# Expert results gathered row by row for each token, and one group's routing held behind two quads of expert tiles

## The chip, the cores and the metric

The kernel runs on one core of a Trainium2 chip (trn2). The metric is device time in microseconds (us) of one launch, as the median of several runs. TensorE (PE) multiplies matrices, VectorE (DVE) and ScalarE (ACT) work on elements, GpSimd (POOL) copies weights and issues indirect DMAs, SyncE (SP) issues the plain ones.

## The reference

Sixteen sequences of 256 tokens with 128 features pass through half a mixture-of-experts layer, an attention layer, and half an expert layer again with the same weights.

```python
x = x + 0.5 * _L0_ffn_ref(_layernorm(x, axis=-1), norm_scale, gate_w, gate_b, w1, b1, w2, b2)
x = x + _L0_attn_ref(_layernorm(x, axis=-1), Wq, bq, Wk, bk, Wv, bv, Wfq, bfq, Wfk, bfk)
x = x + 0.5 * _L0_ffn_ref(_layernorm(x, axis=-1), norm_scale, gate_w, gate_b, w1, b1, w2, b2)

# _L0_ffn_ref, 32 experts, 4 for each token, t the normalized rows
g = t @ gate_w.T + gate_b
vals, idx = jax.lax.top_k(gf, K)
w = jax.nn.softmax(vals, axis=-1)
combine = jnp.zeros((T, E)).at[jnp.arange(T)[:, None], idx].add(w)
h1 = jnp.einsum('th,efh->tef', tf, w1) + b1
h = _swiglu(h1)
out = jnp.einsum('tef,ehf->th', h * combine[:, :, None], w2) + combine @ b2
return x + out
```

## The kernel before

The 4096 tokens form two groups of four blocks; a block (`TB`) is four token tiles of 128 tokens. Each group goes through the layer twice with experts: `first[g]` and `last[g]` hold the state of the first and the second pass (tile names end in `_f` and `_l`).

**Routing.** `route` normalizes a block, computes the gates, finds the best four experts, and keeps the mask `m`, the rank of each token among those of its tile that chose the same expert (`rank`), and the weights (`combT`). `dispatch` turns the counts into places: each expert's tokens of one tile are put into rows of five (`RB = 5`), a row of 640 floats being one unit of the scratch memory `xs` (sorted inputs) and `ys` (expert outputs). One-hot matmuls (line 677) build the rows and one indirect DMA a token tile (line 596, on POOL) scatters 128 rows of 2560 bytes.

**Experts.** `experts` walks over 23 quads (`NQS`) of four expert tiles of 25 rows each. For a quad it loads `xq` (line 710, SP), copies the four tiles' first weights from the resident `w_sb` into the buffers `w1` (line 717, POOL, five buffers, two used by a quad), transposes `xq`, multiplies (`ph`, line 737), applies the gate function on ACT and DVE (lines 741, 742, 747), multiplies again (`po`, line 755), and stores `ys` (line 762, SP). After each quad it calls `beside`, which takes a few steps of another generator.

**Beside.** `groups` runs four expert passes, each next to one chain: `enter(1)` (route and dispatch group 1), `middle(0)` and `middle(1)` (combine the first pass, attention, route and dispatch the second pass), `leave(0)` (combine the second pass and store). `leave(1)` comes last, next to nothing. The number of steps a quad is 3, 3, 3, 2. Inside a chain, `staggered` starts the blocks some steps apart.

```python
beside = [enter(1, clear), middle(0), middle(1), leave(0)]
steps = [3, 3, 3, 2]
for i in range(2 * n_grp):
    waiting.append(beside[i])
    st = first[i] if i < n_grp else last[i - n_grp]
    experts(st, 0, nq, lambda: step(steps[i]))
    finish()
waiting.append(leave(1))
finish()
```

**Combine.** `combined` gathers, for each token tile, the tile's 128 rows of `ys` with one indirect DMA (line 786, POOL, four buffers `gt` of 128 x 640 floats). On PE it forms the places of all pairs in the rows (`pa`, lines 798 and 799) and the weights (`pwb`, line 800), on DVE ten weighted one-hot matrices `u` (line 809), and it multiplies them with the gathered rows: five `pu` matmuls a token tile (line 816) and one for the biases `b2` (line 819). The residual is added at line 822. It is called for every block of both passes.

The order in which the instructions of an engine are issued is fixed when the kernel is built: the framework takes those that are ready by its own estimates, earlier written ones first, and adds the semaphores. The last part of the kernel, under `tc.If`, is a second run for token counts that don't fit into 23 quads; it does not run with these inputs.

Of the kernel before, what the change touches and what calls it, by code (L numbers as in the profile page):

```python
# [13 lines left out]
I32 = mybir.dt.int32  # L14
AF = mybir.ActivationFunctionType
# [7 lines left out]
P = 128  # L23
NJ = 4
# [22 lines left out]
NB = NT * BT  # L47
LIMIT = 7.0
# [3 lines left out]
NONE = -1.0e38  # L52
ROUND = 8388608.0
# [3 lines left out]
def kernel(  # L57
# [144 lines left out]

    ones = const.tile([P, P], BF16, tag="ones", name="ones")
# [197 lines left out]
    class Group:  # L401


        def __init__(self, g, name):
            self.g, self.name = g, name
            self.blocks = []
            self.n = grp.tile([P, GB], BF16, tag="n", name=f"n_{name}", bufs=3)
            self.row = grp.tile([P, 2, GJ], U32, tag="row", name=f"row_{name}", bufs=3)
# [5 lines left out]
        def enter(self, b):  # L414
            self.blocks.append(Block())
            self.held(b, "tn", [P, NJ, P], F32, GB + 1)
            self.blocks[b].xr = dram.tile(
                [P, NJ * P], F32, tag=f"xr_{self.name}{b}", name=f"xr_{self.name}{b}"
            )

            self.held(b, "rank", [P, P], BF16, 2 * GB + 2)
            self.held(b, "combT", [P, P], F32, 2 * GB + 2)
            return self.blocks[b]

        def sort(self, b):
            self.held(b, "seg", [P, P], F32, 2 * GB + 2)
            self.held(b, "seg_b", [P, P], BF16, 2 * GB + 2)
            self.held(b, "off", [P, P], BF16, 2 * GB + 2)
            return self.blocks[b]
# [14 lines left out]
    def route(st, src, b, co):  # L444
# [11 lines left out]
        pt = transposed(tn, f"pt_{name}")  # L456
# [18 lines left out]
        for j in range(NJ):  # L475
# [3 lines left out]
        comb = small.tile([P, NJ, NE], F32, tag="comb", name=f"comb_{name}")  # L479
# [9 lines left out]
            upto_self.rearrange("p c t -> p (c t)"), start=True, stop=True,  # L489
        )  # L490
# [35 lines left out]
    def dispatch(st, clear=False):  # L526
# [45 lines left out]
        )  # L572
        pick = small.tile([P, GB, 2 * NJ], F32, tag="pick", name=f"pick_{name}")
# [116 lines left out]

    def loaded(tab, q, engine, top):
        _, vals = nc.values_load_multi_w_load_instructions(
            tab[0:1, q * NJ : (q + 1) * NJ], engines=[engine],
            min_val=0, max_val=top, skip_runtime_bounds_check_because="made on the chip from at most NE - 1",
        )
        return vals

    def experts(st, lo, hi, beside):
# [28 lines left out]
        def first(q):  # L727
# [4 lines left out]
            for c in range(2):  # L732
                ph = ps_h.tile([P, 2, 2, P], F32, tag="ph", name=f"ph_{name}_{q}_{c}")
                ts = slice(2 * c, 2 * c + 2)
                for s in range(2):
                    for part in range(2):
                        nc.tensor.matmul(  # L737
                            ph[:, part, s, 0:RT], w_q[c][:, s, part * P : (part + 1) * P],
                            x_q[:, 2 * c + s, :], start=True, stop=True,
                        )  # L740
# [33 lines left out]
    def combined(st, b, tag):  # L774
# [47 lines left out]
        nc.vector.tensor_tensor(r, pu, xr, ALU.add)  # L822
        yield r
# [116 lines left out]

    first, last = {}, {}
# [21 lines left out]
    def routes(g, gap, most):  # L963
# [6 lines left out]
        yield  # L970

# [174 lines left out]
```

## Time and profile before

| | |
|---|---|
| median of 3 runs | 738.46 us (733.2 to 739.15) |
| profiled execution | 734.1 us, of which the span of the trace is 732.0 us |
| PE, DVE, ACT, POOL busy | 620.1, 483.1, 379.5, 284.5 us |
| mean granted clock of PE | 0.938 |
| first and last `ph_f` matmul | 99.6 and 378.8 us |
| first and last `ph_l` matmul | 407.2 and 683.1 us |
| gathers (line 786) | 64, 0.94 to 1.44 us each on POOL |
| scatters of rows (line 596) | 64, and 9 that clear rows |
| weight copies (line 717) | 368, 0.416 us in the mean |

An engine's busy time is what its instructions take; waiting at a semaphore is not in it. For an indirect DMA the entry on POOL is the issuing of it, not the transfer. A PE matmul of 32-bit floats shows as two records here (320 records of line 816 for the 160 matmuls of two groups). A row of a timeline gives start, duration, engine, line, operation, what is written and read, and in brackets the idle time ahead of it with what ended it.

### The profile page before, as it was taken

The numbers are of one execution on the slowest core, as the hardware profiler recorded it, in microseconds if no ns is written. First come the engines' busy times: TensorE is split into PE (matmuls) and PEld (weight loads), VectorE is DVE, ScalarE is ACT, GpSimd is POOL, SyncE is SP. The second block draws the span as 40 slices with busy tenths as digits, with TensorE's granted clock in tenths as the row PEclk, the third lists the DMA queues.
The fourth block names the chain that finished last, engine by engine and source line by source line (L and its number), as shares of the span: only waits on it lengthen the run. The fifth ranks groups of instructions, "written<-read, shape, count | busy, mean of one in ns | idle before, by whom it ended". The sixth has DMA issues, their size and how long they took to land.

```text
span 732.0 us, 15990 instructions
## 1 busy us (share of the span) xinstructions
PE 620.1 (85%) x4897; PEld 574.3 (78%) x4897; DVE 483.1 (66%) x1823; ACT 379.5 (52%) x902; POOL 284.5 (39%) x567
## 2 busy tenths in 40 slices
PE   3677489979978988988997998988889789999595
PEld 1466389878978977977896887877789689999585
DVE  6863975855555688887774469888878535554443
ACT  2753376735543766864552455775655335445210
POOL 3023424467645422122365532402227645434242
PEclk9887779999999999998999999999999989999989
DMA  7999346477656435124355644513434667765463
GB/s 229 374 336 328 138 139 172 128 259 227 193 157 198 128 90 140 48 81 128 112 197 194 185 119 124 143 44 85 129 100 174 215 182 213 199 189 160 111 204 118
DMA packets 132695, 122.45 MB, mean 167 GB/s; under 512 B 9626, under 2 KB 118714, under 8 KB 132602
## 3 DMA queue, kind: packets, MB, share of 16 engines
q1 hardware_dynamic: 117658, 71.62, 34.6%
q0 software_dynamic: 10960, 44.90, 18.2%
q10 hardware_dynamic: 3984, 4.82, 1.8%
q8 instruction: 43, 0.70, 0.4%
q14 instruction: 50, 0.41, 0.2%
HBM read 57.78 MB, written 63.52 MB: 166 GB/s over the span
## 4 chain that ended last, share of the span: by engine, by line
PE 53%; DVE 21%; DMA 11%; ACT 7%; issue 6%; POOL 1%; another core or an unknown queue 0%; SPq 0%; POOLq 0%; ACTq 0%; DVEq 0%
PE ph_l L737 8%; PE ph_f L737 7%; PE p_l L677 4%; PE pu_f L816 4%; PE po_l L755 4%; PE po_f L755 4%; PE p_f L677 3%; PE pu_l L816 3%; DMA xs<-s_f,row_f 3%; PE pxT_l L723 2%; DMA gt_l<-ys,row_l 2%; DMA xq_l<-xs 1%; DMA w_sb<-in_w_dram 1%; PE pxT_f L723 1%; DVE lin_f L742 1%
## 5 line engine op out<-in xcount | busy, mean ns | idle before, releaser
L717 POOL COPY w_l<-w_sb 128x256 f32 x184 | 71.3, 416 | 124.4 <-PE ph_l L737 118.6
L717 POOL COPY w_f<-w_sb 128x256 f32 x184 | 70.3, 414 | 117.7 <-PE ph_f L737 116.2
L737 PE MATMUL ph_f<-xT_f,w_f 128*128 128x125 f32 x736 | 97.7, 281 | 1.4 <-DVE lin_f L742 1.1
L737 PE MATMUL ph_l<-xT_l,w_l 128*128 128x125 f32 x736 | 95.5, 279 | 0.1
L737 PEld LDWEIGHTS ph_f<-xT_f,w_f 128*128 128x128 f32 x736 | 90.9, 197 | 2.4 <-POOL w_f L717 1.4
L737 PEld LDWEIGHTS ph_l<-xT_l,w_l 128*128 128x128 f32 x736 | 89.6, 196 | 0.6 <-issue 0.3
L742 DVE TENSOR_SCALAR lin_l<-ph_l 128x250 f32<-128x250 f32 x92 | 37.8, 413 | 53.8 <-ACT a_l L741 53.3
L742 DVE TENSOR_SCALAR lin_f<-ph_f 128x250 f32<-128x250 f32 x92 | 37.5, 412 | 37.3 <-ACT a_f L741 36.2
L816 PE MATMUL pu_l<-gt_l,u_l 128*128 128x128 f32 x320 | 46.2, 290 | 11.5 <-DMA gt_l<-ys,row_l 7.5
L816 PEld LDWEIGHTS pu_l<-gt_l,u_l 128*128 128x128 f32 x320 | 42.7, 203 | 16.8 <-issue 9.8
L677 PE MATMUL p_f<-tn_f,o_f 128*128 128x128 f32 x320 | 46.3, 303 | 10.2 <-DVE rank_f L438 4.1
L677 PEld LDWEIGHTS p_f<-tn_f,o_f 128*128 128x128 f32 x320 | 43.1, 214 | 14.1 <-DVE rank_f L438 4.2
L816 PE MATMUL pu_f<-gt_f,u_f 128*128 128x128 f32 x320 | 45.7, 284 | 7.3 <-DMA gt_f<-ys,row_f 5.6
L755 PE MATMUL po_f<-w_sb,a_f 128*125 x368 | 49.9, 278 | 1.3 <-DVE a_f L747 0.9
L755 PE MATMUL po_l<-w_sb,a_l 128*125 x368 | 49.3, 277 | 1.4 <-DVE a_l L747 0.8
L741 ACT ACTIVATE a_l<-ph_l 128x250 f32<-128x250 f32 x92 | 34.7, 379 | 29.2 <-PE ph_l L737 25.1
L596 POOL DMA_INDIRECT xs<-s_f,row_f x32 | 31.3, 977 | 45.4 <-ACT s_f L682 23.4
L786 POOL DMA_INDIRECT gt_l<-ys,row_l x32 | 30.6, 958 | 44.2 <-PE pu_l L816 23.6
L816 PEld LDWEIGHTS pu_f<-gt_f,u_f 128*128 128x128 f32 x320 | 40.3, 194 | 9.3 <-DMA gt_f<-ys,row_f 5.2
L741 ACT ACTIVATE a_f<-ph_f 128x250 f32<-128x250 f32 x92 | 34.5, 381 | 23.8 <-PE ph_f L737 18.7
L755 PEld LDWEIGHTS po_f<-w_sb,a_f 128*125 128x125 f32 x368 | 45.0, 191 | 1.7 <-ACT yq_f L760 1.0
L755 PEld LDWEIGHTS po_l<-w_sb,a_l 128*125 128x125 f32 x368 | 44.9, 191 | 1.6 <-ACT yq_l L760 1.0
(339 smaller groups left out, 1456.9 us busy)
## 6 DMA issues: line engine op xcount, KB each, us to landing
xq_f<-xs SPq DMA_DIRECT2D x46, 224.0 KB
ys<-yq_f SPq DMA_DIRECT2D x46, 224.0 KB
xq_l<-xs SPq DMA_DIRECT2D x46, 224.0 KB
ys<-yq_l SPq DMA_DIRECT2D x46, 224.0 KB
xs<-zero SPq DMA_DIRECT2D x14, 500.0 KB
w_sb<-in_w_dram SPq DMA_DIRECT2D x4, 1024.0 KB
ys<-zero SPq DMA_DIRECT2D x2, 1250.0 KB
x<-in_x_dram SPq DMA_DIRECT2D x8, 256.0 KB
```

The lines of the kernel that those rows point to most:

```text
L596: ins = nc.gpsimd.indirect_dma_start(out=xs[st.g][:, :], out_offset=bass.IndirectOffsetOnAxis(ap=index, axis=0), in_=rows.rearrange("p r h ...
L677: nc.tensor.matmul(p0[:, r, :] if r < 4 else p1[:, 0:P], o[:, r, :], k.tn[:, t, :], start=True, stop=True,)
L717: nc.gpsimd.tensor_copy(w[:, s, :], w_flat[:, bass.ds(at[2 * c + s], 2 * P)])
L723: nc.tensor.transpose(pt[:, t, 0:RT], xq[:, t, :], ident[:RT, :RT])
L737: nc.tensor.matmul(ph[:, part, s, 0:RT], w_q[c][:, s, part * P : (part + 1) * P], x_q[:, 2 * c + s, :], start=True, stop=True,)
L741: nc.scalar.activation(a[:, ts, :], ph[:, 0, :, 0:RT], AF.Silu, scale=ALPHA)
L742: nc.vector.tensor_scalar(lin[:, ts, :], ph[:, 1, :, 0:RT], LIMIT + 1.0, 1.0 - LIMIT, ALU.min, ALU.max,)
L755: nc.tensor.matmul(po[:RT, t, :], hT[:, t, :], w_flat[:, bass.ds(at[t] + 2 * P, P)], start=True, stop=True,)
L786: nc.gpsimd.indirect_dma_start(out=gt.rearrange("p r h -> p (r h)"), out_offset=None, in_=ys[st.g][:, :], in_offset=bass.IndirectOffsetOnA ...
L816: nc.tensor.matmul(pu[:, t, :], u[:, r, s, :], got[t][:, r, :], start=(r == 0), stop=False)
```

## The change

A second way to combine, `gathered`, is used in `middle(0)`, `middle(1)` and `leave(0)`; `leave(1)` keeps `combined`. A row of `ys` is now taken as five rows of 128 floats, one for each token and expert. For every token tile four indirect DMAs fetch the 128 tokens' four result rows (512 bytes each) into `gt`; DVE multiplies each by its weight and adds it to the residual, four operations a token tile. On PE only the `b2` matmuls stay.

The row numbers and weights come from a new generator, `places`. `route` keeps each token's rank in token order (one more matmul and one more DVE operation a block; unchosen experts get 0, chosen ones their rank plus 16384). `places` adds the place of the (tile, expert) pair's first row, takes the four largest values with MAX8, and picks the weights by comparison. `mixed` runs one of its four steps within every fourth step of `enter(1)` (for `first[0]`) and every sixth step of `middle` (for `first[1]` and `last[0]`).

In `routes` the second group's chain yields six times (two quads' worth) before its first block, and that block's first transposes are placed behind the last `ph` matmul of the quad with number 1 (`HELD`). Some buffers that only `combined` of earlier groups needed are fewer.

```diff
+    HELD = 1
+    issued = {}
...
+        nc.tensor.matmul(
+            prank[:, 2 * P : 3 * P], upto_self[:, 0, :], m.rearrange("p j e -> p (j e)"),
+            start=True, stop=True,
+        )
+        nc.vector.scalar_tensor_tensor(
+            st.rk[:, b, :], prank[:, 2 * P : 3 * P], CHOSEN, m.rearrange("p j e -> p (j e)"),
+            ALU.add, ALU.mult,
+        )
...
-        pt = transposed(tn, f"pt_{name}")
+        if name == "f10":
+            with tc.issue_after(issued[f"f0_{HELD}"].ins):
+                pt = transposed(tn, f"pt_{name}")
+        else:
+            pt = transposed(tn, f"pt_{name}")
...
+    def places(st):
+        name = st.name
+        st.row_k = grp.tile([P, GJ, TOPK], U32, tag="row_k", name=f"row_k_{name}")
+        st.w_k = grp.tile([P, GJ, TOPK], F32, tag="w_k", name=f"w_k_{name}")
+        base = small.tile([P, GB], F32, tag="base", name=f"base_{name}")
+        nc.vector.tensor_tensor(base, st.at, st.lo, ALU.add)
+        nc.vector.tensor_scalar(base, base, float(RB), -1.0 - CHOSEN, ALU.mult, ALU.add)
+        for b in range(GB):
+            js = slice(b * NJ, (b + 1) * NJ)
+            work = tmp.tile([P, RB, 2, P], F32, tag="u", name=f"work_{name}{b}", bufs=2)
+            diag, d = work[:, 0, 0, :], work[:, 0, 1, :]
+            found = work[:, 1:3].rearrange("p a c (k e) -> p (a c) k e", k=TOPK)
+            nc.vector.tensor_scalar(diag, ident, base[:, b : b + 1], None, ALU.mult)
+            pd = bank(f"pd_{name}{b}")
+            nc.tensor.matmul(pd[:, 0:P], ones_f, diag, start=True, stop=True)
+            nc.vector.tensor_tensor(d, pd[:, 0:P], st.rk[:, b, :], ALU.add)
+            d = d.rearrange("p (j e) -> p j e", j=NJ)
+            d8 = small.tile([P, NJ, 8], F32, tag="d8", name=f"d8_{name}{b}")
+            for j in range(NJ):
+                nc.vector.max(d8[:, j, :], d[:, j, :])
+            nc.vector.tensor_copy(st.row_k[:, js, :], d8[:, :, 0:TOPK])
+            nc.vector.tensor_tensor(
+                found, d.unsqueeze(2).to_broadcast([P, NJ, TOPK, NE]),
+                d8[:, :, 0:TOPK].unsqueeze(3).to_broadcast([P, NJ, TOPK, NE]), ALU.is_equal,
+            )
+            nc.vector.tensor_tensor(
+                found, found, st.cw[:, b].unsqueeze(2).to_broadcast([P, NJ, TOPK, NE]), ALU.mult
+            )
+            nc.vector.tensor_reduce(st.w_k[:, js, :], found, AX.X, ALU.add)
+            yield
+
+    def mixed(main, other, every):
+        for i, _ in enumerate(main):
+            if i % every == every - 1:
+                next(other, None)
+            yield
+        yield from other
...
+    def gathered(st, b, tag):
+        name = f"{st.name}{b}"
+        k = st.blocks[b]
+        rows = ys[st.g].rearrange("n (r h) -> (n r) h", r=RB)
+        xr = tmp.tile([P, NJ, P], F32, tag="xr", name=f"xri_{name}", bufs=3)
+        nc.sync.dma_start(xr.rearrange("p j h -> p (j h)"), k.xr)
+        got = []
+        def get():
+            j = b * NJ + len(got)
+            gt = tmp.tile([P, RB, P], F32, tag="gt", name=f"gt_{st.name}{j}", bufs=4)
+            for i in range(TOPK):
+                nc.gpsimd.indirect_dma_start(
+                    out=gt[:, i, :], out_offset=None, in_=rows,
+                    in_offset=bass.IndirectOffsetOnAxis(ap=st.row_k[:, j, i : i + 1], axis=0),
+                )
+            got.append(gt)
+        get()
+        get()
+        comb4 = split(k.combT, F32, nc.scalar, "comb4", name, 2)
+        yield
+        pu = bank(f"pu_{name}").rearrange("p (j h) -> p j h", j=NJ)
+        for t in range(NJ):
+            nc.tensor.matmul(pu[:, t, :], comb4[:, t, :], b2_sb, start=True, stop=True)
+        r = tmp.tile([P, NJ, P], F32, tag=tag, name=f"{tag}_{name}", bufs=3)
+        nc.vector.tensor_tensor(r, pu, xr, ALU.add)
+        get()
+        yield
+        for t in range(NJ):
+            for i in range(TOPK):
+                nc.vector.scalar_tensor_tensor(
+                    r[:, t, :], got[t][:, i, :], st.w_k[:, b * NJ + t, i : i + 1], r[:, t, :],
+                    ALU.mult, ALU.add,
+                )
+            if len(got) < NJ:
+                get()
+            yield
+        yield r
...
+        if g and not run_name:
+            for _ in range(6):
+                yield
...
     def enter(g, clear):
-        yield from routes(g, 2, 2)
-        yield from dispatch(first[g], clear)
+        def chain():
+            yield from routes(g, 2, 2)
+            yield from dispatch(first[g], clear)
+        yield from mixed(chain(), places(first[0]) if g else iter(()), 4)
...
     def middle(g):
-            for x1 in combined(first[g], b, "x1"):
+            for x1 in gathered(first[g], b, "x1"):
...
-        yield from staggered((block(b) for b in range(GB)), 9, 3, True)
-        yield from dispatch(last[g])
+        def chain():
+            yield from staggered((block(b) for b in range(GB)), 9, 3, True)
+            yield from dispatch(last[g])
+        yield from mixed(chain(), places(last[0] if g else first[1]), 6)
...
     def leave(g):
-            for y in combined(last[g], b, "x1"):
+            for y in (combined if g else gathered)(last[g], b, "x1"):
```

More of the change, by code (lines that the diff above doesn't have):

```diff
@@ L47 @@
 NB = NT * BT
+assert NB * RB < 16384
 LIMIT = 7.0
@@ L201 @@
     nc.vector.tensor_scalar(place_f, step_f, self_f, None, ALU.add)
+    ones_f = const.tile([P, P], F32, tag="ones_f", name="ones_f")
+    nc.gpsimd.memset(ones_f, 1.0)
     ones = const.tile([P, P], BF16, tag="ones", name="ones")
@@ L736, in first @@
                     for part in range(2):
-                        nc.tensor.matmul(
+                        issued[f"{name}_{q}"] = nc.tensor.matmul(
                             ph[:, part, s, 0:RT], w_q[c][:, s, part * P : (part + 1) * P],
```

20 lines of the change are left out of this document (14 added, 6 removed).

## The prediction

> **What bounds the kernel now.** I read the page's busy shares first, then its groups, then the busy time cut at the stage borders, then the timelines of GpSimd (POOL) and TensorE (PE) where the change lands. The borders come from the first and last `ph_f` and `ph_l` matmuls and from the last `x_f` of each middle stage. The 208.5 to 407 stretch is called stage 2 (group 1's first expert pass beside `middle(0)`), 407 to 593 stage 3 (beside `middle(1)`), 593 to 686 stage 4 (beside `leave(0)`); the rest is the tail, `leave(1)`.
>
> ```profile
> PE 620.1 (85%) x4897; PEld 574.3 (78%) x4897; DVE 483.1 (66%) x1823; ACT 379.5 (52%) x902; POOL 284.5 (39%) x567
> ...
> L717 POOL COPY w_l<-w_sb 128x256 f32 x184 | 71.3, 416 | 124.4 <-PE ph_l L737 118.6
> ...
> L816 PE MATMUL pu_l<-gt_l,u_l 128*128 128x128 f32 x320 | 46.2, 290 | 11.5 <-DMA gt_l<-ys,row_l 7.5
> ...
> L786 POOL DMA_INDIRECT gt_l<-ys,row_l x32 | 30.6, 958 | 44.2 <-PE pu_l L816 23.6
> ```
>
> PE leads over the whole run, and POOL mostly waits for it: 118.6 us of its waits end with `ph_l`. An average hides the stages, so the next view gives busy time by stretch (length, then PE, weight loads, DVE, ACT, POOL, with their counts, granted clock, DMA).
>
> ```profile
> 208.50:308.00 99.50, 87.83 (x712) 81.63 (x713) 72.63 (x301) 60.81 (x137) 34.24 (x66) 0.98 0.46 129
> 308.00:407.00 99.00, 83.74 (x658) 78.43 (x657) 68.13 (x261) 49.45 (x122) 40.41 (x72) 0.92 0.47 145
> 407.00:498.00 91.00, 84.01 (x668) 78.33 (x668) 70.06 (x295) 57.95 (x136) 27.59 (x59) 0.95 0.40 113
> 498.00:593.00 95.00, 79.24 (x643) 73.23 (x643) 69.40 (x265) 48.46 (x119) 40.67 (x67) 0.96 0.49 153
> 593.00:686.00 93.00, 92.15 (x803) 90.62 (x802) 47.88 (x100) 47.39 (x108) 39.18 (x91) 0.98 0.62 173
> ```
>
> Stage 4 is wholly PE's: 92.15 of 93 us. In the first halves of stages 2 and 3, where all gathers of the old combine sit, PE is busy 88% and 92%, and VectorE (DVE) already 73% and 77%.
>
> **What the change takes away.** In 12 of 16 blocks (all but `leave(1)`) the one-hot combine goes. On PE, the timeline has the 10 `pu` records of a token tile in 1.12 us, so 4 x 1.12 = 4.5 us a block; the two `pa` and the `pwb` matmuls take about 1.5 us more (235.8 to 237.3). That is 6.0 us a block, 24 us a stage. DVE loses 10 `u` operations, in runs of four in 1.40 us, so 3.5 us, and one 0.70 us split: 4.2 us a block, 17 us a stage. ACT loses a 0.59 us copy a block, off the path.
>
> **What it adds on POOL.** Each token tile had one indirect DMA of 128 rows of 2560 B; now it has four of 128 rows of 512 B. That is 64 a stage for 16. This row type back to back on POOL shows the price:
>
> ```profile
> 691.62 0.94 POOL L786 DMA_INDIRECT gt_l<-ys,row_l  x1 [0.30 <-issue]
> 692.87 0.95 POOL L786 DMA_INDIRECT gt_l<-ys,row_l  x1 [0.30 <-issue]
> 694.12 0.95 POOL L786 DMA_INDIRECT gt_l<-ys,row_l  x1 [0.30 <-DMA gt_l<-ys,row_l]
> ```
>
> The step from one to the next is 1.25 us, and 1.27 among the scatters. No row shows a 512 B gather. Upper bound: the longest here, 1.44 and a 0.30 gap, 1.74 us. Lower bound: if 0.95 us goes by bytes, a fifth of it, 0.19, and the gap, 0.49 us. I take 1.27, because the number of rows, 128, is the same, and the scatters and gathers of this trace, alike in rows but not in direction, cost the same to 0.03 us. So a stage needs 64 x 1.27 = 81 us of POOL for gathers. To it come the weight copies of line 717: a quad of expert tiles needs four in 1.65 us, 23 quads 38 us. They wait behind the gathers in POOL's order, and PE's `ph` waits for them.
>
> **What it adds on DVE and PE.** Per block, 16 multiply-adds of 128x128, each reading the row the last one wrote: nearest is line 636, 0.36 to 0.39 us, so 0.40 with the gap that dependent DVE steps show (232.69, 232.88, 233.08): 6.4 us a block. Bounds: 0.28 (line 499) to 0.51 (line 502 when stretched). `places` costs, per block, 0.3 (diagonal, as line 635) + 0.3 (add) + 0.5 (four MAX8) + 0.25 (cast) + 3 x 0.69 (three 512-wide operations, as lines 822 and 831) = 3.4 us, so 14 us in each of stages 1 to 3, the first steps of the stage. `route` has one more 0.28 us operation a block. In the first half of stage 2 DVE then has 72.6 - 17 + 25.6 + 13.7 + about 0.5 = 95 us to do in 99.5. PE gets a 0.23 us matmul and a bf16 one of about 0.11 us a block: 1.4 us a stage. The gathers move 4.2 MB a stage where it was 5.2, in rows of 512 B; the transfer queues are at a 0.4 to 0.6 share there, so I put this at nothing, and up to 4 us of landing (3.58 us at 690.3) where POOL has no lead.
>
> A rule against it: the Trainium skill, "SBUF — State Buffer", section "Who interferes with whom", says that a DVE instruction with two SBUF inputs and a GpSimd instruction that reads SBUF shut each other out. The new multiply-adds are of that kind; the old `u` took one input from PSUM. Weight copies here take 0.37 us alone in a pair (0.74) and 0.416 in the mean, so some of it may be here already. If a fifth of 64 operations, POOL's copy share of such a stage, each held a copy for 0.40 us, that would be 5 us a stage and a total some 15 us higher. I add nothing for it.
>
> **Stage by stage.**
> - *Head of stage 1, -4 us.* The second group's routing is traced two quads later, and its first transposes stand behind the second quad's last `ph`.
>
> ```profile
> 90.70 1.15 PE L292 MATMUL pt_f<-ident,tn_f 128*128 128x128 f32 x4 [7.57 <-DVE tn_f L451]
> 92.80 1.91 PE L462 MATMUL pgate_f<-gate_sb,tT_f 128*128 128x32 f32 x8 [0.95 <-ACT tT_f L458]
> 94.53 1.09 PE L292 MATMUL pt_f<-ident,tn_f 128*128 128x128 f32 x4
> 95.41 1.04 PE L723 MATMUL pxT_f<-ident,xq_f 125*128 125x125 f32 x4
> ```
>
> PE stands 7.57 us for a transpose while the first quad's `xq_f`, issued at 85.86, is on its way. The chain shows such loads landing in 5.1 to 5.6 us, so at 91.2; `ph` could start at 92.8 and not at 99.4. The 25 records moved behind cost some 2.8 us later (0.112 each). So 6.6 - 2.8 = 4 us gained. Bounds: -7, and +2 if the load lands late. The route chain (its `xr_f` stores on ACT's queue, 0.33 us each, and the scatters of line 596) comes 6 us later; the cover is 190 to 208, where bare quads run. SP's queue keeps its order there. `places` has the slack of DVE: 69 us busy of 109.
> - *Stage 2, +6 us.* POOL paces the first half: from the first gather at 214.7, 81 us and twelve quads of copies, 20 us, then landing and adding, 5 us: 320 for the last `x1`, where it was 308. DVE alone, 95 us at nine tenths busy, says 106 us for 99.5. Of the 12 us lost about half comes back, since PE has 23 us less work. Bounds -12 and +12.
> - *Stage 3, +6 us.* Gathers can begin at 389.9, so POOL has a lead, and says 390 + 5 (four scatters) + 81 + 17 (two quads' copies are made early) + 5 = 498, as now; DVE says 93 us for 91, some 10 more at nine tenths. The last scatter of `dispatch` now has two gathers ahead of it at 389.9 and 395.1; two or three more are 3 us. Bounds -12 and +14.
> - *Stage 4, +15 us.* PE falls from 93 to 23 x 3.09 + 4 = 75 us (3.09 is the step of bare quads, 669.04 to 672.13). POOL needs 81 + 38 = 119 us, of which some 18 fit between 575.6, when the results have landed, and 593. If gathers always give way, POOL ends at 593 + 101 = 694, +8. If the program's order holds, 16 quads take 81 + 26 - 18 = 89 us and seven more run at 3.09: 593 + 89 + 22 = 704, +18 and more where a gather waits for one of the four `gt` buffers. I take +15.
> - *Tail: nothing.* `leave(1)` is as before, as long as POOL is done with stage 4's gathers when it starts.
>
> Sum: -4 + 6 + 6 + 15 = +23. The profiled execution took 734.1 us (span 732.0), 4.4 below the median of 738.46 and inside the runs' 733.2 to 739.15: 757 us.
>
> **Rivals.** (1) *A 512 B gather is cheap on POOL.* At 0.49 us stage 4 needs 31 + 38 = 69 us of POOL, below PE's 75: -18 there. In stages 2 and 3 DVE's 95 and 93 us then decide: nothing gained. With the head: 734.1 - 22 = 712. For: nothing here prices such rows. Against: equal prices for equal row counts. It decides below about 0.6 us. (2) *PE's time comes back.* The order is packed so that half of the 24 us returns in stages 2 and 3 (-12 each), stage 4 costs +8, the head -4: 714. For: over 208.5 to 686, POOL's total, 182 us busy, 24 of gaps (80 indirect DMAs) and 144 x 1.27 = 183 more, is 389 of 478. Against: the gathers stand in first halves. (3) *Blocked gathers hold the queue.* Gathers of this trace wait 49 us for PE to free buffers, 34 times, 1.4 us each; DVE frees them now, later. If each of the 36 tiles beyond the first four of a stage costs 1.4 us, all while copies stand behind, POOL loses 50 us; half of it reaches the end: 757 + 25 = 782. (4) *The hold does nothing*, since `xq_f` lands after 97: 761.
>
> **How the numbers follow.** Forecast 0.52, rival 1 0.10, rival 2 0.18, rival 3 0.12, rival 4 0.08. The half-widths of the four stages' bounds (5, 12, 13, 9), added as squares, make 20: the forecast's own range is 737 to 777. Leaving out the lower part of rivals 1 and 2 and the upper of 3 gives 716 to 784. About 1% is what a measurement of this kernel tells from no change, 731 to 746: faster 0.27, within 0.13 (0.10 from the forecast's low end, 0.03 from rival 2), slower 0.60.
>
> **What would show it.** POOL's busy time near 284 + 144 x 0.95 = 421 us, and 0.9 of its time in the first 16 quads of stage 4; 192 gathers at 0.9 to 1.0 us; weight copies ended less by `ph` and by POOL's own queue, with `ph` waiting for `w_f` and `w_l`; PE's total near 550 us; first `ph_f` near 93; DVE over 90% early in stages 2 and 3. The forecast is wrong if gathers show under 0.6 us, if stage 4 is shorter than 93 us, or if the stretch to the last `x_f` is under 90 us.

## The result and the profile after

The changed kernel takes 865.1 us (863.2 to 869.0), against 737.5 us for the kernel before in the same series: a ratio of 1.175, with a 95% interval of 1.168 to 1.181. The forecast was 757 us. The direction was right, the size was not: +128 us where the sum had +23.

All medians and ratios below are against runs of the kernel before on the same chip; its own median moved between 730 and 740 us from series to series, so ratios are compared, not times.

First the page of the changed kernel: PE's busy share, the slices of PE, POOL and PE's granted clock, and the groups of gathers (line 902), weight copies (line 781) and multiply-adds (line 923).

```profile
PE 597.2 (69%) x4407; PEld 551.5 (64%) x4409; DVE 525.2 (61%) x2025; ACT 369.6 (43%) x890; POOL 433.4 (50%) x712
...
PE   4596589889545672869882585658889536787976
...
POOL 3034233676674737112467786451225668885242
PEclk9798699999855975799995696869998858698989
...
L902 POOL DMA_INDIRECT gt_f<-ys,row_k_f x128 | 127.8, 998 | 51.6 <-issue 32.6
L781 POOL COPY w_f<-w_sb 128x256 f32 x184 | 71.7, 424 | 128.4 <-PE ph_f L801 121.9
L781 POOL COPY w_l<-w_sb 128x256 f32 x184 | 71.5, 421 | 90.4 <-PE ph_l L801 66.8
L902 POOL DMA_INDIRECT gt_l<-ys,row_k_l x64 | 62.5, 977 | 16.6 <-issue 16.0
L923 DVE SCALAR_TENSOR_TENSOR x_f<-gt_f,w_k_f,x_f 128x128 f32<-128x128 f32 x128 | 43.5, 362 | 23.9 <-DMA gt_f<-ys,row_k_f 19.7
L923 DVE SCALAR_TENSOR_TENSOR x_l<-gt_l,w_k_l,x_l 128x128 f32<-128x128 f32 x64 | 24.9, 401 | 44.8 <-DMA gt_l<-ys,row_k_l 35.4
```

PE's share fell from 85% to 69%, and no engine is full: POOL is at 50% over the run. A gather costs what the forecast took (0.98 to 1.00 us, and the gap behind it). The slices show the pattern: early in stages 2 and 3 (from the 11th and the 22nd slice on), where POOL mostly reads 6 to 8, PE reads as low as 2 and its clock falls to 5 or 6. Later in the stage they change places: PE reads 8 or 9, POOL 1 or 2. The copies still mostly wait for `ph` (121.9 and 66.8 us).

PE's own waits for the first product show which queue PE saw ahead of it (total, times, longest):

```profile
PE ph_l L801 <- DVE lin_l L806: 39.3, 14, 8.6
...
PE ph_f L801 <- DVE lin_f L806: 16.4, 7, 6.0
...
PE ph_l L801 <- POOL w_l L781: 6.6, 2, 5.0
```

`lin` is DVE's first step on the expert tiles; until it has read an earlier `ph`, a later one has no room. So in this kernel PE stands mostly behind DVE, and seldom for a weight copy by name. The experiments show that the one wait hides the other.

Next, the busy time cut at the borders of the stages, halved as before (length, PE, weight loads, DVE, ACT, POOL with counts, granted clock, DMA share, GB/s).

```profile
217.50:345.00 127.50, 67.24 (x421) 61.28 (x419) 63.19 (x247) 39.54 (x96) 78.30 (x108) 0.68 0.30 84
345.00:464.60 119.60, 90.64 (x727) 85.08 (x728) 91.80 (x390) 61.30 (x156) 45.22 (x78) 0.90 0.36 115
464.60:585.00 120.40, 73.76 (x501) 68.94 (x501) 73.50 (x300) 45.49 (x110) 75.62 (x108) 0.77 0.30 84
585.00:688.20 103.20, 81.07 (x660) 75.83 (x659) 75.49 (x306) 59.59 (x150) 41.36 (x70) 0.93 0.42 134
688.20:813.50 125.30, 88.41 (x631) 85.71 (x631) 55.25 (x127) 41.29 (x93) 86.94 (x138) 0.81 0.46 128
```

In the first half of stage 2, POOL is busy 78.3 us; with the gap of 0.30 us behind each of 64 gathers that makes 97.5 of 127.5. So 30 us pass in which POOL does nothing, while PE works for only 67 us at a clock of 0.68.

From the first `ph` of each pass, the stages are, in us (d is the kernel with one gather a token tile, e the one without weight copies, q the one with spread gathers and free additions, v the one with two gathers a token tile; all below). Each row is one profiled execution, and they come from several chips, so a difference of two or three us is not read.

| | head | stage 1 | stage 2 | stage 3 | stage 4 | tail | span |
|---|---|---|---|---|---|---|---|
| before | 99.6 | 111.9 | 195.7 | 185.9 | 90.3 | 48.6 | 732.0 |
| changed | 98.2 | 119.3 | 247.1 | 223.6 | 125.3 | 47.8 | 861.3 |
| d | 99.2 | 115.6 | 198.4 | 186.1 | 78.8 | 48.6 | 726.7 |
| e | 96.2 | 115.4 | 198.4 | 189.1 | 106.5 | 49.8 | 755.4 |
| q | 97.7 | 118.3 | 206.8 | 202.5 | 128.4 | 48.0 | 801.8 |
| v | 99.0 | 115.8 | 197.7 | 185.5 | 90.1 | 48.9 | 737.0 |

**One burst of gathers.** The timeline of the changed kernel in stage 2 shows 32 gathers from 221.88 to 264, with six weight copies (one and a half quads' worth) between the sixteenth and the seventeenth:

```profile
241.06 0.94 POOL L902 DMA_INDIRECT gt_f<-ys,row_k_f  x1 [0.30 <-issue]
242.00 2.10 POOL L781 COPY w_f<-w_sb 128x256 f32 x6
244.26 0.98 POOL L902 DMA_INDIRECT gt_f<-ys,row_k_f  x1 [0.16 <-issue]
```

The same time in stretches of 10 us:

```profile
220.00:230.00 10.00, 6.73 (x61) 6.43 (x59) 4.59 (x15) 3.74 (x8) 6.62 (x8) 1.00 0.47 126
230.00:240.00 10.00, 1.29 (x5) 0.93 (x6) 4.82 (x14) 0.57 (x1) 7.57 (x9) 0.52 0.39 105
240.00:250.00 10.00, 6.67 (x30) 6.02 (x30) 5.04 (x15) 0.38 (x1) 8.32 (x13) 0.50 0.16 48
250.00:260.00 10.00, 3.03 (x13) 2.48 (x12) 1.98 (x9) 0.38 (x1) 7.56 (x9) 0.50 0.18 52
260.00:270.00 10.00, 1.88 (x9) 1.88 (x10) 1.04 (x6) 1.62 (x4) 6.58 (x14) 0.50 0.22 65
```

PE does 1.29 us of work in one of these stretches and 1.88 in another. POOL is the only engine that works throughout, on gathers, with the copies behind them in its queue. The first two `ph` groups after PE's long gap from 226.7 us (only two transposes between) show both kinds of wait:

```profile
239.39 2.04 PE L801 MATMUL ph_f<-xT_f,w_f 128*128 128x125 f32 x8 [6.01 <-DVE lin_f L806]
242.46 2.07 PE L801 MATMUL ph_f<-xT_f,w_f 128*128 128x125 f32 x8 [1.03 <-issue]
```

The weights of the first had been copied by 220.3 us; it waited for `lin`, which stood behind multiply-adds that waited for gathered rows. The second started just behind the first of the six copies (242.00 to 242.40). When the copies' turn comes, POOL often waits in turn for `ph` to free their buffers (five, a quad takes two).

### The profile page after: what moved, and what is told of

Read it like the earlier page. It is cut to its first block, busy times and chain, and to the rows that moved or that the text cites. A ratio compares the mean times of both kernels' runs of the same rounds, so it can differ in the third digit from the quotient of the medians.

```text
span 861.3 us, 15492 instructions
## 1 busy us (share of the span) xinstructions
PE 597.2 (69%) x4407; PEld 551.5 (64%) x4409; DVE 525.2 (61%) x2025; ACT 369.6 (43%) x890; POOL 433.4 (50%) x712
## 5 line engine op out<-in xcount | busy, mean ns | idle before, releaser
L801 PE MATMUL ph_l<-xT_l,w_l 128*128 128x125 f32 x736 | 112.6, 309 | 66.5 <-DVE lin_l L806 39.3
L902 POOL DMA_INDIRECT gt_f<-ys,row_k_f x128 | 127.8, 998 | 51.6 <-issue 32.6
L801 PEld LDWEIGHTS ph_l<-xT_l,w_l 128*128 128x128 f32 x736 | 104.3, 223 | 71.7 <-issue 54.7
L781 POOL COPY w_f<-w_sb 128x256 f32 x184 | 71.7, 424 | 128.4 <-PE ph_f L801 121.9
L801 PE MATMUL ph_f<-xT_f,w_f 128*128 128x125 f32 x736 | 106.0, 296 | 42.4 <-DVE mv_a L357 17.7
L801 PEld LDWEIGHTS ph_f<-xT_f,w_f 128*128 128x128 f32 x736 | 97.7, 210 | 46.0 <-issue 43.3
L781 POOL COPY w_l<-w_sb 128x256 f32 x184 | 71.5, 421 | 90.4 <-PE ph_l L801 66.8
L902 POOL DMA_INDIRECT gt_l<-ys,row_k_l x64 | 62.5, 977 | 16.6 <-issue 16.0
L819 PE MATMUL po_l<-w_sb,a_l 128*125 x368 | 57.1, 299 | 5.8 <-DVE a_l L811 4.6
L923 DVE SCALAR_TENSOR_TENSOR x_f<-gt_f,w_k_f,x_f 128x128 f32<-128x128 f32 x128 | 43.5, 362 | 23.9 <-DMA gt_f<-ys,row_k_f 19.7
L923 DVE SCALAR_TENSOR_TENSOR x_l<-gt_l,w_k_l,x_l 128x128 f32<-128x128 f32 x64 | 24.9, 401 | 44.8 <-DMA gt_l<-ys,row_k_l 35.4
L787 PE MATMUL pxT_l<-ident,xq_l 125*128 125x125 f32 x184 | 32.4, 300 | 22.7 <-DMA xq_l<-xs 20.5
```

The costliest lines, as they stand in the source:

```text
L781: nc.gpsimd.tensor_copy(w[:, s, :], w_flat[:, bass.ds(at[2 * c + s], 2 * P)])
L787: nc.tensor.transpose(pt[:, t, 0:RT], xq[:, t, :], ident[:RT, :RT])
L801: issued[f"{name}_{q}"] = nc.tensor.matmul(ph[:, part, s, 0:RT], w_q[c][:, s, part * P : (part + 1) * P], x_q[:, 2 * c + s, :], start=True ...
L819: nc.tensor.matmul(po[:RT, t, :], hT[:, t, :], w_flat[:, bass.ds(at[t] + 2 * P, P)], start=True, stop=True,)
L902: nc.gpsimd.indirect_dma_start(out=gt[:, i, :], out_offset=None, in_=rows, in_offset=bass.IndirectOffsetOnAxis(ap=st.row_k[:, j, i : i + 1 ...
L923: nc.vector.scalar_tensor_tensor(r[:, t, :], got[t][:, i, :], st.w_k[:, b * NJ + t, i : i + 1], r[:, t, :], ALU.mult, ALU.add,)
```

## The experiments: which part costs

Two theories were set against each other first. *P*: weight copies stand behind gathers in POOL's order, and PE waits for them. *D*: multiply-adds that wait for a gather hold DVE, with the expert tiles' `lin` behind them.

**One gather a token tile** (`d_one_gather`; 16 a stage, all else as changed):

```diff
-            for i in range(TOPK):
-                nc.gpsimd.indirect_dma_start(out=gt[:, i, :], ..., in_=rows, in_offset=...row_k[:, j, i : i + 1]...)
+            nc.gpsimd.indirect_dma_start(out=gt.rearrange("p r h -> p (r h)"), ..., in_=ys[st.g][:, :],
+                                         in_offset=...st.row[:, 0, j : j + 1]...)
```

> The changed kernel with one indirect DMA of 128 rows of 2560 bytes for a token tile, as before, in place of four of 512 bytes; the multiply-adds, places, the hold and the PE savings stay (the sums are of other rows, so the values differ). Theories P and D (the number of gathers at 1.25 us is the cause, by either queue): 740 us or less, since PE has lost 70 us of work. Theory V (the DVE work added by places and by 192 multiply-adds is the cause): 800 us or more.

Measured: 731.5 us, ratio 1.002 (0.998 to 1.007). The number of gathers is the whole loss: the multiply-adds, `places`, the hold and the fewer buffers, all still there, cost nothing on balance. But PE's busy time is 565.7 us here for 620.1 before, and little of these 54 us is gained: by the table, stage 4 is 11.5 us shorter (78.8 for 90.3), while stages 2 and 3, where as much of PE's work went, are no shorter and stages 1 to 3 together are 6.6 us longer (the last part returns to this).

**Multiply-adds that wait for no gather** (`c_adds_free`):

```diff
-                    r[:, t, :], got[t][:, i, :], st.w_k[...], r[:, t, :],
+                    r[:, t, :], xr[:, t, :], st.w_k[...], r[:, t, :],
```

> The changed kernel, with one difference: the multiply-adds of gathered read the residual tile xr in place of the gathered rows, so that no DVE instruction waits for a gather; all 192 gathers are still issued (the expert results are left out of the sum). Theory D (DVE stands in its queue at a multiply-add whose gather has not landed, and the gate operations lin that PE needs stand behind it): 760 us or less, stages 2 to 4 some 30 us shorter each. Theory P (weight copies stand behind runs of 16 gathers in POOL's queue, whatever DVE does): 840 us or more. If both weigh alike, about 800 to 820.

Measured: 835.0 us, 1.141 (1.135 to 1.147). Freeing DVE alone gives back 0.034, some 25 us, of the 128. What DVE's waits had hidden shows in PE's waits of this kernel:

```profile
PE ph_l L801 <- POOL w_l L781: 66.3, 15, 12.9
PE ph_f L801 <- POOL w_f L781: 36.6, 4, 14.6
```

PE now waits 103 us for weight copies, where the changed kernel named 6.6. The two waits stand one behind the other, so their prices can't be read from either trace alone.

**No weight copies** (`e_fixed_w`, and `f_fixed_before`, the same edit on the kernel before as a control):

```diff
-            at = loaded(st.at_w, q, POOL, (NE - 1) * EW)
-            ... nc.gpsimd.tensor_copy(w[:, s, :], w_flat[:, bass.ds(at[2 * c + s], 2 * P)])
...
-                            ph[:, part, s, 0:RT], w_q[c][:, s, part * P : (part + 1) * P],
+                            ph[:, part, s, 0:RT], w_sb[:, (4 * q + 2 * c + s) % NE, part * P : (part + 1) * P],
```

> The changed kernel without the 368 weight copies of POOL: the first expert matmul reads the weights of an expert fixed by the quad's number where they lie in w_sb (so the wrong expert's weights). Gathers and multiply-adds stay. Theory P (copies behind gathers starve PE): 780 us or less. Theory D (lin behind multiply-adds that wait for gathers): 840 us or more, for DVE still waits. Both alike: 800 to 830.

> Control for the kernel without weight copies: the kernel before, with the 368 copies left out and the first weights read in place from fixed experts. If the 105 us that the changed kernel got back are the collision of copies with gathers, this one changes little: 722 to 742 us. If the copies cost by themselves, 700 us or less.

Measured: 760.0 us, 1.038 (1.031 to 1.046), for the changed kernel without copies; 721.3 us, 0.983 (0.978 to 0.989), for the kernel before without them. All 192 gathers and their transfers are still there, and DVE still waits 67 us for gathered rows (55 in the changed kernel), yet most of the loss is gone: 0.136, or 100 us, of which 0.017 is what the copies cost in the kernel before. P is shown in this sense: gathers and copies in one queue cost about 88 us that neither costs alone. Against its own control the kernel without copies is still 0.055 slower, some 40 us; by the table 16 of them lie in stage 4 (106.5 for 90.3). Since without copies POOL also has less to do, this does not yet tell order from quantity.

## The experiments: order or quantity

*B*: it is the order, bursts ahead of the copies. *Q*: it is the quantity on POOL.

**Gathers spread** (`n_spread` with the hold, `o_spread_free` without): six a quad (`LOT = 6`), each lot behind that quad's last copy, so POOL's order mostly reads four copies, six gathers, four copies.

```diff
+            with tc.issue_after(issued["copy"].ins):
                 nc.gpsimd.indirect_dma_start(out=gt[:, i, :], ...)
...
-            experts(st, 0, nq, lambda: step(steps[i]))
+            experts(st, 0, nq, lambda: (fetch(LOT), step(steps[i])))
```

> As the changed kernel, hold included, but the same 192 gathers are not written in lots of eight and sixteen: six a quad, each lot behind that quad's last weight copy, so that GpSimd's order is four copies, six gathers, four copies. Number, size and price of gathers and all other work are unchanged. Theory B (the order: bursts of 16 to 24 gathers, 20 to 30 us, stand ahead of the copies that TensorE needs next, and the work itself would fit): six gathers and four copies are 6 x 1.25 + 1.65 = 9.2 us against 8.4 us a quad, so most of the 105 us that the kernel without copies gave back comes here too: 770 to 800 us. Theory Q (the quantity: GpSimd's 240 us of gathers, or their transfers, are too much wherever they stand): 845 us or more.

> The spread gathers, and without the hold and the six yields. Theory B: as above, less what the hold cost (55 us in the bursts; if that was mostly collision with bursts, less): 735 to 765 us. Theory Q: 800 us or more, as without the hold alone (809.6).

Measured: 855.0 us, 1.159 (1.150 to 1.168), and 854.3 us, 1.154 (1.149 to 1.160). B as it was put fell. Why, the timeline of the spread kernel in stage 4 shows:

```profile
677.15 0.94 POOL L906 DMA_INDIRECT gt_l<-ys,row_k_l  x1 [0.30 <-PE ph_l L801]
...
678.03 0.35 DVE L927 SCALAR_TENSOR_TENSOR x_l<-gt_l,w_k_l,x_l 128x128 f32<-128x128 f32 x1 [2.03 <-DMA gt_l<-ys,row_k_l]
...
678.56 0.35 DVE L927 SCALAR_TENSOR_TENSOR x_l<-gt_l,w_k_l,x_l 128x128 f32<-128x128 f32 x1 [0.18 <-issue]
678.83 0.41 DVE L806 TENSOR_SCALAR lin_l<-ph_l 128x250 f32<-128x250 f32 x1
679.39 1.13 PE L801 MATMUL ph_l<-xT_l,w_l 128*128 128x125 f32 x8 [1.45 <-DVE lin_l L806]
```

PE waits for DVE's `lin`; `lin` stands behind multiply-adds; these wait for gathers issued just ahead of them. And from the view of waits of that kernel (total, times, longest):

```profile
DVE x_l L927 <- DMA gt_l<-ys,row_k_l: 53.5, 45, 3.3
...
DVE x_f L927 <- DMA gt_f<-ys,row_k_f: 31.9, 26, 3.0
```

85 us, for 55 in the changed kernel: with the copies out of the way, the wait for rows had grown.

**Spread, with additions that wait for nothing, or come later** (`q_spread_adds_free`: as spread, additions as in `c_adds_free`; `p_spread_lag`: the right rows, a quad later, behind the next quad's `lin`):

```diff
+                with tc.issue_after(issued["lin"].ins):
                     nc.vector.scalar_tensor_tensor(r[:, t, :], got[t * TOPK][:, i, :], ...)
```

> The spread gathers (six a quad behind the quad's copies), and the multiply-adds read the residual tile in place of the gathered rows, so that nothing waits for a gather; the combine adds other numbers. All 192 gathers are issued as in the spread kernel (855.0). Theory D (with the copies out of the way, VectorE's order is what is left: multiply-adds wait 85 us for gathers issued just before them, and the expert tiles' lin stands behind them): 745 to 785 us, by GpSimd's 9.2 us against 8.4 us a quad. Theory Q (the quantity on GpSimd costs wherever it stands and whoever waits): 820 us or more.

> The spread kernel with each token tile's four multiply-adds placed behind the lin of the next quad, one quad after its last gather; same work, same rows. Theory D, held waits of VectorE being what costs: 790 to 825 us. Theory C (the chain sets the stage: the next pass starts a fixed 95 us or so after the last combined block, and that can't come before 64 gathers at 1.25 us and the copies among them are through, some 100 us after the first gather, however VectorE is ordered): 840 to 870 us, since the lag makes the last block no earlier.

Measured: q 804.9 us, 1.098 (1.092 to 1.105); p 829.9 us, 1.132 (1.124 to 1.141). Each lies between what its two theories had. Neither order nor waiting for rows is all: with both removed, q is still 0.098 above before, some 72 us. Its first half of stage 2, and its stage 4:

```profile
216.00:325.00 109.00, 79.59 (x580) 74.78 (x579) 86.66 (x355) 57.38 (x134) 88.77 (x125) 0.87 0.43 115
625.40:753.80 128.40, 90.00 (x623) 87.17 (x623) 45.70 (x106) 42.17 (x89) 96.53 (x146) 0.83 0.50 132
```

With 64 gaps of 0.30 us, POOL has 108.0 us of work in the 109.0 of the first stretch: it is full. In stage 4 it has 115.7 of 128.4. And what PE waits for in q are copies:

```profile
PE ph_l L801 <- POOL w_l L781: 54.3, 17, 5.7
PE ph_f L801 <- POOL w_f L781: 24.5, 9, 5.0
```

Stage 4 of q is no shorter than that of the changed kernel (125.3): there neither order nor waits for rows matter, and the quantity on POOL is what is left. In stages 2 and 3 order and waits cost 40 and 21 us more.

**Two of four gathers** (`v_two_slots`, 32 a stage, order and hold as changed):

```diff
-            for i in range(TOPK):
+            for i in range(0, TOPK, 2):
                 nc.gpsimd.indirect_dma_start(...)
```

> The changed kernel, hold included, with two of the four row gathers a token tile (32 a stage, not 64); the multiply-adds read each fetched row twice, so the combine adds other numbers. With 16 gathers a stage this stood at 731.5, with 64 at 865. Theory L (each gather costs alike): 731 + 134 x 16/48 = 776 us. Theory T (a threshold: 40 us of gathers and 38 of copies are 78 us a stage and find room, bursts of 10 us are covered by the copies made ahead): 735 to 755 us.

Measured: 740.1 us, 1.019 (1.012 to 1.026). Theory T holds. With 16, 32 and 64 gathers a stage the ratios are 1.002, 1.019 and 1.175: the second sixteen cost 0.017 and the last thirty-two 0.156, so there is no fixed price for each. Its rows for the first half of stage 2 and for stage 4:

```profile
214.70:315.00 100.30, 74.81 (x539) 70.02 (x537) 83.45 (x347) 54.30 (x129) 54.04 (x87) 0.86 0.35 96
597.90:688.00 90.10, 76.25 (x632) 74.65 (x631) 52.80 (x121) 41.35 (x92) 56.05 (x106) 0.93 0.55 154
```

POOL has 64 of 100 us to do (54.0 and 32 gaps), and bursts of eight are covered by copies made ahead: PE waits for copies 4.4 us in the whole run. Stage 4 is as long as before (90.1 for 90.3), and with 16 gathers a stage it was 78.8: in that stage PE's saving shows as far as POOL has room.

**The last stage alone** (`r_leave_all`: row gathers only in `leave(0)`; `s_leave_one`: only in its first block; no hold, the old combine elsewhere):

```diff
-            for y in (combined if g else gathered)(last[g], b, "x1"):
+            for y in (gathered if last[g].keep and b < 1 else combined)(last[g], b, "x1"):
```

> Row gathers and places for the second pass of the first group alone (the four blocks of leave(0)); both middles keep the old combine, no hold. To make room some buffers are fewer (8 in place of 10 of the routing tiles). Theory Q4 (beside bare expert tiles GpSimd's 64 gathers and 92 copies, 118 us, are the bound, with little lead): the last stage grows by 20 to 36 us, 755 to 775 us in all. The prediction's term alone (+15, with 18 us of lead): 745 to 753 us. Theory D4 (the last stage only suffered from what came late out of the stages before it): 730 to 742 us.

> The same for the first block of leave(0) alone: 16 row gathers and 12 old ones. Its gathers fit into the 17 us in which GpSimd stands idle ahead of the last expert pass, and TensorE loses 6 us of work in a stage that it fills (92 of 93 us). Theory Q4 (only what GpSimd can't hide costs): 4 to 7 us below before, 728 to 732. If every row gather costs its 1.25 us: 15 us above, 750.

Measured: 771.9 us, 1.058 (1.051 to 1.064), with a stage 4 of 122.6 us for 90.3; and 741.6 us, 1.015 (1.009 to 1.021). The first confirms that stage 4 loses by itself, with nothing late out of the stages before; that it loses by quantity is q's part. The second was expected as a gain and is a loss, between the two theories: its second quad starts 9.3 us after the first (591.7 to 601.0, of which 6.0 waiting for `lin`), not 3, and stage 3, which has `places` beside it and fewer buffers, takes 190.4 us and not 185.9. Which of the two is at fault there was not separated.

## The experiments: the hold

**The hold away, and the hold alone** (`a_no_hold`, from the changed kernel; `b_hold_only`, onto the kernel before; `j_one_no_hold`, from the kernel with one gather a tile):

```diff
-        if name == "f10":
-            with tc.issue_after(issued[f"f0_{HELD}"].ins):
-                pt = transposed(tn, f"pt_{name}")
...
-        if g and not run_name:
-            for _ in range(6):
-                yield
```

> The changed kernel without the hold: the second group's routing starts at once and its first transposes have no edge to the first two quads. Theory H (the hold, by making ACT and DVE keep the second group's coefficients ahead of the first quad, costs the 6 us by which stage 1 ends later): 3 to 8 us faster than the changed kernel. Rival (the 6 us are the DVE work of places inside the coefficient chain, 90.0 to 94.5 us): within 3 us of the changed kernel.

> The kernel before with the hold and the six yields alone; the old combine stays. Theory H1: 750 to 790 us, 20 to 55 above before. Theory H2, and the prediction's term for the head: 727 to 737 us, a gain of 0 to 4 us.

> One 2560-byte gather a token tile (16 a stage, not 64; it leaves out fetching the four chosen rows, so the combine adds other numbers), and no hold, no six yields. With the hold this was 731.5. Theory H1 (the hold costs by itself, through the order it leaves on SyncE's and ScalarE's queues): 680 to 710 us. Theory H2 (the hold only costs when it meets bursts of gathers): 722 to 738 us.

Measured: a 809.6 us, 1.105 (1.099 to 1.110); b 742.8 us, 1.003 (1.000 to 1.007); j 728.8 us, 0.987 (0.982 to 0.993). In the changed kernel the hold costs 0.070, some 52 us, two fifths of the loss; in the kernel before, nothing that can be told; with one gather a tile 0.015, some 11 us. With spread gathers (n against o) it costs 0.005, inside the intervals. So most of it is a loss by meeting the bursts, not by itself.

Both theories for a fell short. Stage 1 does end 7.6 us sooner without the hold (209.9 for 217.5 us), as the first had it. But stages 2 and 3 are 27 and 16 us shorter as well (219.9 and 207.2), which neither had.

POOL's order is nearly the same with and without the hold. One thing that differs in stage 2 is SyncE's queue, seen in the timeline of the changed kernel (an SPq row is an issue, with the time that the queue stood at it):

```profile
233.40 34.38 SPq L774 DMA_DIRECT2D xq_f<-xs  x2
268.09 0.81 SPq L826 DMA_DIRECT2D ys<-yq_f  x2
```

and beside it on ScalarE and PE:

```profile
267.48 0.58 ACT L824 COPY yq_f<-po_f 125x512 f32<-125x512 f32 x1 [12.35 <-remote]
...
268.12 2.07 PE L819 MATMUL po_f<-w_sb,a_f 128*125 x8 [10.35 <-ACT yq_f L824]
```

Loads of `xq` stand for 34 us, a store of results behind them; ACT's copy and PE's second product wait at the same time. In the view of waits of the changed kernel, loads stand 84.5 us, in seven waits, for something of which the profile has no record; the changed kernel without the hold has no such wait (the spread kernels have 26 us with the hold and 23 without). So the stores were moved:

**Stores of the results on ScalarE's queue** (`t_ys_act` from the changed kernel, `z_no_hold_ys_act` without the hold as well, `x_before_ys_act` from the kernel before):

```diff
-                nc.sync.dma_start(ys_q[q]...[rows], yq[rows])
+                nc.scalar.dma_start(ys_q[q]...[rows], yq[rows])
```

> The changed kernel, with the stores of the expert results (ys<-yq) issued from ScalarE's queue and not from SyncE's, where loads of xq that wait up to 33 us stand ahead of them. Theory S (this is where the hold's 55 us went: a late load holds a store, the store the copy out of the second product, that TensorE): 805 to 840 us. Rival: the loads are late because TensorE is, and the stores cost nothing: 855 to 875 us.

> The changed kernel without the hold and the six yields, and with the stores on ScalarE's queue. Theory S (the hold's 55 us are what the order of loads and stores on SyncE's queue cost): both together give little more than either alone (809.6 and 825.4): 800 to 820 us. Rival (two separate losses): 865 - 55 - 40 = 770 us.

> The kernel before with the stores of the expert results on ScalarE's queue. In the changed kernel this gave back some 40 us, where loads of xq held the stores. Theory S: in the kernel before no load of xq waits that long, so this changes nothing: 727 to 741 us. If the stores cost on SyncE's queue anyway: 715 us or less, and then a version better than both.

Measured: t 825.4 us, 1.126 (1.118 to 1.133); z 818.1 us, 1.120 (1.114 to 1.126); x 739.3 us, 1.012 (1.007 to 1.017). As a table of ratios:

| changed kernel | stores on SyncE | stores on ScalarE |
|---|---|---|
| with the hold | 1.175 | 1.126 |
| without | 1.105 | 1.120 |

With the stores off SyncE's queue the hold costs 0.006, with them on it 0.070: one loss, not two. By themselves the stores are better where they were (x, and z against a). That the held store is the link is what the table shows; what ended the load's wait is not, since the profile names no releaser for it and PE shows no record between 258 and 268 us.

**All repairs together** (`w_repaired`: spread, additions a quad later, stores on ScalarE's queue, no hold):

> All repairs at once: gathers spread six a quad, multiply-adds a quad later, stores of the results on ScalarE's queue, no hold. If the repairs act on different waits: 785 to 815 us. If they all act on the same lateness: 820 to 835, as the spread with the lag alone (829.9). In no case below before, since 64 gathers a stage still set GpSimd's 9.2 us a quad and the last stage.

Measured: 821.8 us, 1.128 (1.122 to 1.134), as p alone. So the repairs act on the same lateness, as the second theory had it, and the quantity on POOL stays. No kernel that fetches four rows a token tile throughout and adds them came below 1.10, and no version that keeps the whole computation came below the kernel before.

## Why the prediction was wrong, by its own steps

- **Price of a gather: right.** 0.94 us and a 0.30 gap for 512-byte rows, as for rows of 2560. POOL's total of 433 us answers to 421. Rival 1 is out.
- **Head, -4: +6.** The `xq_f` load did land early (89.4 us), but the first `ph` moved only from 99.6 to 98.2:

```profile
89.39 1.06 PE L787 MATMUL pxT_f<-ident,xq_f 125*128 125x125 f32 x4 [5.73 <-DMA xq_f<-xs]
...
94.65 2.03 ACT L539 ACTIVATE xr_f<-x,co_f 128x128 f32<-128x128 f32 x5 [11.60 <-DVE co_f L398]
96.69 0.57 ACT L789 COPY xT_f<-pxT_f 128x500 f32<-128x500 f32 x1
...
97.32 1.09 PE L787 MATMUL pxT_f<-ident,xq_f 125*128 125x125 f32 x4 [6.87 <-ACT xT_f L789]
98.21 3.18 PE L801 MATMUL ph_f<-xT_f,w_f 128*128 128x125 f32 x16
```

  The wait passed to ACT, where `xr_f` of the held block stands ahead of the copy that the first `ph` needs. The step looked at PE's queue and not at ACT's. In the kernel with the hold alone, which has no `places` to delay DVE's `co_f`, the `xr_f` run from 91.3 us, three us sooner, thirteen of them ahead of the copy, and its first `ph` is at 98.2 too. Stage 1 is then 7 us longer: the last scatter comes at 204.4 us for 192.0, so the "cover" from 190 to 208 was the way to the next pass. The hold is what does it, not `places`: stage 1 ends at 218.4 us in the kernel with the hold alone, 217.5 in the changed kernel and 209.9 in the changed kernel without the hold.
- **Stages 2 and 3, +6 each: +51 and +38. This is the step that failed.** It added POOL's work of a half-stage (81 + 20 + 5 us) as if the queue worked through without a pause, priced the order of the queues at nothing, and let half of the excess come back later. In q, where nothing waits for gathers, POOL is indeed full, with 108 us, and the stages lose 11 and 17 us. The other 40 and 21 are order and waits: in the changed kernel bursts and waits take turns, and the last combined block of stage 2 came at 372.1 us, not 320. And hardly anything comes back: from the last combined block to the next pass's first `ph` it is 98.2 and 95.8 us in the two middles before, 92.5 and 94.5 changed, 94.6 and 94.6 in q, 93.6 and 95.2 in v (85 to 92 in p and w, whose additions come a quad later). Attention, routing and dispatch of the last block are a chain of nearly fixed length, and PE's 24 us less work is not in it: with one gather a token tile stages 2 and 3 are 198.4 and 186.1 us, for 195.7 and 185.9 before. Where the chain sets a stage, a us of delay of the last block is nearly a us of the end.
- **Stage 4, +15: +35.** POOL's 119 us were right. The +15 lay between an order in which gathers give way (+8) and the order as written (+18), and the written order holds: some 20 gathers stand at its head, and two fifths of the copies, 36, stand behind the last gather. That comes at 779.3 us, 91 after the stage's first `ph` (the working had 89), but nine quads follow it in 34 us and not seven in 22. Its other assumption, that PE's 24 us come back here, is right only where POOL has room (78.8 us with 16 gathers).
- **Tail, nothing: right** (47.8 us for 48.6).
- **Rival 2** (PE's time comes back) is out, by the chain above and by the kernel with one gather a token tile. **Rival 3** put blocked gathers ahead of copies: the place was right, the mechanism was not. Gathers idle for 68 us in all, of which 49 are the gaps between them; they seldom wait, they run, and the copies wait. **Rival 4** was nearest for the head, but the loads were not late.
- **PE's total near 550: 597**, and the matmuls are 4407 for 4897, as the change has it. PE was slower, not busier: the mean granted clock was 0.844 for 0.938. **DVE over 90%: no**, 63 of 127 us in the first half of stage 2; it waited more than it worked. The three signs of being wrong that the prediction named all lay on the side of a shorter time, and none of them came.
- **The rule of the Trainium skill on DVE and GpSimd** ("SBUF — State Buffer", "Who interferes with whom") was weighed and left at nothing. Copies take 424 and 421 ns here for 414 and 416, some 3 us over 368 of them. It is DVE that is held: one multiply-add, at 242.37 us beside the six copies from 242.00 to 244.10, took 1.87 us where the median is 0.35. That agrees with the rule, and costs little in this case: over the 192 multiply-adds (mean 362 and 401 ns) it makes some 5 us.

## What to carry to other kernels

A sum of work by engine and stage holds only where that queue never waits for the engine that it feeds: write the queue's order down, and ask what the next consumer needs and how many items are ready ahead of it. Here the copies made ahead covered bursts of eight gathers; with sixteen, once DVE's waits were out of the way, PE waited up to 14.6 us for a copy. Before pricing a wait, ask what stands right behind it: here freeing one queue only uncovered the other. Find the chain that sets a stage's end before letting saved work of a busy engine count as a gain: in these middles PE's 24 us were worth nothing, and a us of the last combined block was worth nearly a us.

## What the runs showed of the hardware

The time that an indirect gather holds POOL did not depend on the bytes of its rows: 128 rows of 512 B took 0.94 us, and of 2560 B 0.94 to 0.95 in the rows that the prediction shows. Whether it goes by the number of rows is not shown, since every gather here has 128. The Trainium skill, "Perfetto Trace Analysis", section "What "DMA-bound" means", says that where the issuing engine is the bound, large descriptors are what matter. These rows agree, since five times the bytes cost POOL nothing more, and the change went the other way.

A starved PE is also a slow one. In the changed kernel, 16 records of `ph` took 1.95 us in a stretch with a granted clock of 1.00, and 8 took 2.04 after waits, in a stretch with 0.50:

```profile
223.47 1.95 PE L801 MATMUL ph_f<-xT_f,w_f 128*128 128x125 f32 x16
...
255.73 2.04 PE L801 MATMUL ph_f<-xT_f,w_f 128*128 128x125 f32 x8 [4.74 <-issue]
```

The Trainium skill, "TensorE: Matmul & The Clock Gate", section "Part 1: The HAM clock gate", states that the array goes to half rate after an idle window of about 3.4 us. These rows agree: PE's waits of 4.74 to 6.01 us in this burst not only stop it, they halve the speed of what follows. The forecast priced the quads of stage 4 by a step of 3.09 us, taken where the clock was 0.98.
